# A four-layer graph network: ten of the sixteen diagonal blocks in the last layer, and one accumulator pool shared by the last two layers

## The chip, the cores and the metric

The kernel runs on one core of a Trainium2 chip. The metric is the device time of one execution in microseconds; the kernel before takes 1385.57 us (median of three runs, 1384.66 to 1387.64). A change of less than 0.2% (2.8 us) is about what these measurements cannot tell from none.

## The reference, cut to what matters

The input is x (4096 nodes, 64 features) and a symmetric, sparse adjacency matrix adj (4096 x 4096). Four layers follow one another, each of the form `x = layernorm(x + layer(x, adj))`: a polynomial in adj, an attention layer with two gated cells, a decay layer, and a hyperbolic layer. The change touches the last two.

```python
# layer 2 (decay): weight by the number of non-zeros that follow in the row
support = x @ weight
mask = (adj != 0)
rank = cumsum(mask, axis=1); deg = rank[:, -1:]; k = minimum(deg, 100)
pos = rank - (deg - k)
w = mask * where(pos > 0, 0.5 ** (k - pos), 0.0)
out = w @ support + bias

# layer 3 (hyperbolic)
log_ij = logmap(x[:, None, :], x[None, :, :])      # for every pair of nodes
agg = einsum('ij,ijc->ic', adj / deg, log_ij)
transformed = agg @ weight + bias
out = expmap(0, transformed)                        # needs the norm of each row of transformed
```

In the last layer a pair (i, j) needs one scalar factor f(i, j), which the kernel gets from a product of the two nodes' features by a square, three logarithms and exponentials and a few elementwise steps. The factor is symmetric, f(i, j) = f(j, i).

## The kernel before, in words

Nodes are cut into blocks of 128 (`P`) and groups of four blocks, 512 nodes (`GW`); there are 32 blocks and 8 groups. A shared scheduler places the instructions of each engine; `in_order` and `behind` pin the order of those that they name. Buffers come from pools. A pool in PSUM, the matrix engine's result memory, has a number of buffers for each tile name, and the framework adds the waits by which a buffer is not overwritten while it is read.

**The decay layer** (L1455 to L1549). A step counts, for 64 columns of the mask and 512 rows of each of four groups, how many non-zeros follow, and turns each count into a power of two. The loop at L1497 runs over 64 half-blocks `h`, and it is gone through twice (`turns_of`, four groups each), so there are 128 steps, or 64 pairs of an odd and an even step. One step does this:

- for `a` in 0, 1: two matmuls (`r` in 0, 1) of the constant `follow` with the mask write the two partition halves of the count tile `cnt[a]` (L1506); then `cnt[a]` is read out of PSUM into `wt[odd][a]`, by ACT (L1511) for `a == 0`, and for `a == 1` by ACT while there is work of the previous layer or turn to do beside it (`busy`), else by DVE (L1513);
- after these four matmuls come the gathers of earlier steps (L1514): at odd `h` the eight `gather_two` matmuls (L1466), at even `h` the eight `gather_lo` matmuls (L1478). They multiply the weights by the features into four accumulators `acc`.
- at even `h` one step of `seam` follows, a list of small steps of the neighbouring layers (products, transposes, layer norms).

PE runs its instructions in the order in which they stand: count pair `a = 0`, count pair `a = 1`, gathers, then the next step. The two count tiles are two separate tiles of the pool `ps_c2`, `cnt_ps0` and `cnt_ps1`, each 128 x 512 in fp32 with one buffer. After the last step the remaining gathers are run (L1547) and the accumulators are copied out (L1536).

**The last layer** (L1568 to the end). 36 tiles (i, j) of two groups each cover the upper triangle of the matrix of groups, the eight diagonal ones included. A tile is worked in two units `n` of two blocks by 512 columns (128 x 1024 values), so there are 72 units. The functions for a unit are `product` (L1613, PE into the PSUM tile `v_ps`, for even n from the pool `ps_v3`, for odd n from `ps_u3`), `square` (ACT, L1635), `less_one` (DVE, L1657), then in the loop Ln and Exp on ACT (L1866, L1867), `opposite` (PE, L1646), a step on DVE from `v_ps` (L1889), a third Exp and a second Ln on ACT (L1891, L1900), the factor f on DVE (L1876), and its product with the adjacency tile on DVE (L1879). `gather` (L1694, L1706) multiplies the weighted tile by the features. For a tile off the diagonal, `turn` transposes f on PE (L1678) and DVE multiplies the transposed blocks with the mirrored adjacency tile (L1680).

On a diagonal tile (i = j) `columns` makes the second unit half as wide: of the sixteen 128 x 128 blocks the first unit computes eight (two rows of four), the second the four at the lower right. The four at the lower left are transposes of four of the first unit, made by one `turn` (L1671, L1673) one unit later.

When a group's sums are complete, its end is added to `seam` by `finals` (L1770): small steps `first` to `fifth`, one each unit. `third` (L1804) takes the squared norms of the rows with four ACT squares of 64 columns that also sum (L1808). The last two groups' ends stand after the last unit.

Of the kernel before, what the change touches and what calls it, by code (L numbers as in the profile page):

```python
# [9 lines left out]
F32 = mybir.dt.float32  # L10
# [50 lines left out]
def gnn4_kernel(  # L61
# [153 lines left out]
    def in_order(ins):  # L215
        return tc.keep_in_program_order(ins)

    def cols(b):
        return slice(b * P, (b + 1) * P)
# [1171 lines left out]
    def behind(engine, ins):  # L1391

        if engine in begun:
            tc.add_manual_dep(
                ins.ins, begun[engine],
                mybir.DependencyInfo(mybir.DependencyClass.NoSync, mybir.DependencyReason.DATA),
                reason="behind",
            )
        begun[engine] = ins.ins.name
# [52 lines left out]
            lambda ps_p, g=g: turn_prepared(ps_p, g) for g in two  # L1452
        ]

    with tc.tile_pool(name="mask2", bufs=3) as mk_p, tc.tile_pool(name="wt2", bufs=3) as wt_p, tc.tile_pool(  # L1455
        name="ps_c2", bufs=1, space=PSUM
    ) as ps_c, tc.tile_pool(name="ps_p2", bufs=2, space=PSUM) as ps_p, ExitStack() as ps_a_open:

        def masks2():
            return [mk_p.tile([P, CB, GW], MASK, name=f"m{n}") for n in range(2 * QG)]  # L1460
# [24 lines left out]
        gathers = []  # L1485
        busy = True
        for turn, groups in enumerate(turns_of):
            cnt = [ps_c.tile([P, GW], F32, name=f"cnt_ps{a}") for a in range(2)]
            if turn:
                acc = [ps_a.tile([P, GW], F32, name=f"acc_ps{q}") for q in range(QG)]  # L1490
                to_right, to_other, spread, wh_x = constants3()
# [5 lines left out]
            for h in reversed(range(2 * NB)):  # L1497
# [29 lines left out]
                ]  # L1527
                lo = [lambda half=half, jb=jb, wt=wt, acc=acc: gather_lo(jb, half, wt, acc) for half in (1, 0)]

                gathers += lo + two if jb == 0 else two + lo  # L1530
                if jb == 0:
                    def copies(ps_p, acc=acc, groups=groups, turn=turn):
# [32 lines left out]

    with tc.tile_pool(name="ps_v3", bufs=1, space=PSUM) as ps_v, tc.tile_pool(  # L1568
        name="ps_p3", bufs=3, space=PSUM
    ) as ps_p, tc.tile_pool(name="ps_u3", bufs=1, space=PSUM) as ps_u, tc.tile_pool(name="o3", bufs=1) as op, tc.tile_pool(name="cols3", bufs=3) as cols_p, tc.tile_pool(  # L1570
        name="w3", bufs=4
    ) as wp3, tc.tile_pool(name="el3", bufs=3) as el, tc.tile_pool(name="f3", bufs=2) as fp, tc.tile_pool(
        name="r3", bufs=2
    ) as rp, tc.tile_pool(
        name="ps_a3", bufs=1, space=PSUM
    ) as ps_a:
        HB = CB // 2

        tb = op.tile([P, N], F32, name="tb")
        two_w = op.tile([P, 2 * F], F32, name="two_w")  # L1580
        spread_w = two_w[:, F : 2 * F]
        kappa = op.tile([P, 2, NB], F32, name="kappa")

        tiles = [(i, j) for n, i in enumerate(seq) for j in seq[n:]]
        NT = len(tiles)
        own, mirrored = {}, {}
        nc.gpsimd.memset(tb[F:P, gcols(seq[0])], 0.0)
        for g in seq[1:]:
# [11 lines left out]
                mirrored[t] = cols_p.tile([P, CB, GW], F32, name="at_m", tag="atm")  # L1600
                nc.sync.dma_start(mirrored[t], adj_t[j][:, i * CB : (i + 1) * CB, :])

        def columns(n):

            i, j = tiles[n // 2]
            return slice(2 * P if i == j and n % 2 else 0, GW)

        sums, fs = {}, {}
        ros.append(op.tile([P, GW], BF16, name="ro1"))
        vs, ws, rts = {}, {}, {}  # L1610
        NU = 2 * NT

        def product(n):  # L1613

            if n >= NU:
                return
            i, j = tiles[n // 2]
            vs[n] = (ps_u if n % 2 else ps_v).tile([P, HB, GW], F32, name="v_ps")
            cs = columns(n)
            for k in range(HB):  # L1620
                jb = j * CB + (n % 2) * HB + k
                half = slice(jb % 2 * F, jb % 2 * F + F)
                ins = nc.tensor.matmul(  # L1623
                    vs[n][:, k, cs], lhsT=tr_c[half, jb // 2, :], rhs=rights[i][0][half, cs], start=True, stop=True
                )
                in_order(ins)
                if n < 2:
                    behind("PE", ins)

        def square(n):  # L1630
            if n >= NU:
                return
            ws[n] = wp3.tile([P, HB, GW], F32, name="w3")
            cs = columns(n)
            ins = nc.scalar.activation(ws[n][:, :, cs], vs[n][:, :, cs], AF.Square)  # L1635
            behind("ACT", ins)

        def opposite(n):
            if n >= NU:
                return  # L1640
            i, j = tiles[n // 2]
            cs = columns(n)
            for k in range(HB):
                jb = j * CB + (n % 2) * HB + k
                half = slice(jb % 2 * F, jb % 2 * F + F)
                ins = nc.tensor.matmul(  # L1646
                    vs[n][:, k, cs], lhsT=tr_o[half, jb // 2, :], rhs=rights[i][1][half, cs],
                    start=False, stop=True, skip_group_check=True,
                )
                in_order(ins)  # L1650
                if n < 1:
                    behind("PE", ins)

        def less_one(n):
            if n < NU:
                w = ws[n][:, :, columns(n)]
                ins = nc.vector.tensor_scalar(  # L1657
                    w, w, -SCALE * SCALE, V_FLOOR * (V_FLOOR + 2.0) * SCALE**2, ALU.add, ALU.max
                )
                behind("DVE", ins)  # L1660

        def turn(n):

            t, h = n
            i, j = tiles[t]
            work = []
            if i == j:
                tp = ps_p.tile([P, GW], F32, name="post", tag="post")
                for k in range(HB):
                    for b in range(HB):  # L1670
                        nc.tensor.transpose(tp[:, cols(HB * k + b)], fs[t][:, b, cols(HB + k)], ident)  # L1671
                to = own[t][:, HB:CB, 0 : HB * P]
                work.append(lambda: nc.vector.tensor_tensor(to, tp.rearrange("p (k i) -> p k i", k=HB), to, ALU.mult))  # L1673
                return work
            for b in (HB * h, HB * h + 1):
                tp = ps_p.tile([P, GW], F32, name="post", tag="post")
                for k in range(CB):
                    nc.tensor.transpose(tp[:, cols(k)], fs[t][:, k, cols(b)], ident)  # L1678
                to = mirrored[t][:, b, :]
                work.append(lambda to=to, tp=tp: nc.vector.tensor_tensor(to, tp, to, ALU.mult))  # L1680
            return work
# [88 lines left out]
        def finals(g):  # L1770
# [33 lines left out]
            def third(ps_p):  # L1804

                sq = sm.tile([P, GB, F], F32, name="sqv", tag="t0")
                for b in range(GB):
                    nc.scalar.activation(sq[:, b, :], v[:, b, :], AF.Square, accum_out=n[:, b : b + 1])  # L1808
                nc.vector.tensor_scalar_max(n, n, MIN_NORM * MIN_NORM)
                nc.scalar.activation(n, n, AF.Ln)  # L1810
                nc.scalar.activation(vn[:, :, 0], n, AF.Exp, scale=0.5)
                nc.scalar.activation(vn[:, :, 1], n, AF.Exp, bias=ln_two, scale=-0.5)
# [32 lines left out]
        for t in range(3):  # L1845
            load_own(t)
            load_mirrored(t)
        product(0)
        square(0)
        product(1)  # L1850
        less_one(0)
# [2 lines left out]
        while n < NU + 2 or turns or gathers:  # L1854
# [5 lines left out]
            if n < NU:  # L1860
                if n % 2 == 0:
                    fs[n // 2] = fp.tile([P, CB, GW], F32, name="f3")
                w, cs = ws[n][:, :, columns(n)], columns(n)
                rts[n] = el.tile([P, HB, GW], F32, name="rt3")
                rt = rts[n][:, :, cs]
                behind("ACT", nc.scalar.activation(w, w, AF.Ln))  # L1866
                behind("ACT", nc.scalar.activation(rt, w, AF.Exp, scale=0.5))  # L1867
                square(n + 1)
                opposite(n + 1)
            if n >= 2 and n - 2 < NU:  # L1870
                m = n - 2
                t, h = divmod(m, 2)
                cm = columns(m)
                hs = slice(h * HB, (h + 1) * HB)
                f, at = fs[t][:, hs, cm], own[t][:, hs, cm]
                behind("DVE", nc.vector.scalar_tensor_tensor(  # L1876
                    f, rts.pop(m)[:, :, cm], T_MAX, ws.pop(m)[:, :, cm], ALU.min, ALU.mult
                ))
                behind("DVE", nc.vector.tensor_tensor(at, at, f, ALU.mult))  # L1879
                diagonal = tiles[t][0] == tiles[t][1]  # L1880
                before = t - 1 if t and tiles[t - 1][0] != tiles[t - 1][1] else None
                gathers[n + 1] = (t, h, before)
                if diagonal and h == 0:
                    late_turns[n + 1] = (t, 0)
                if not diagonal and h == 1:
                    turns.setdefault(n + 1, []).append((t, 0))
                    turns.setdefault(n + 2, []).append((t, 1))
            if n < NU:
                behind("DVE", nc.vector.scalar_tensor_tensor(rt, vs[n][:, :, cs], (1.0 + V_FLOOR) * SCALE, rt, ALU.max, ALU.add))  # L1889
                product(n + 2)  # L1890
                behind("ACT", nc.scalar.activation(w, w, AF.Exp, scale=-0.5))  # L1891
            late = turn(late_turns.pop(n)) if n in late_turns else []
# [3 lines left out]
            for work in turned + late:  # L1896
                behind("DVE", work())
            if 0 < n <= NU:
                rt = rts[n - 1][:, :, columns(n - 1)]
                behind("ACT", nc.scalar.activation(rt, rt, AF.Ln, scale=1.0 / SCALE))  # L1900
            if n == NU - 6:
                seam += [ahead_of_last(g) for g in seq[-2:]]
# [60 lines left out]
```

## Time and profile before

| | us |
|---|---|
| Median of three runs | 1385.57 (1384.66 to 1387.64) |
| The profiled execution, its own time | 1386.67 |
| Its span, first to last instruction | 1384.9 |
| Decay layer, first count to first product of the last layer | 751.7 to 955.6 |
| Last layer's loop | 955.6 to 1357.0 |
| End of the last two groups | 1357.0 to 1384.9 |
| Busy over the whole span: PE, DVE, ACT | 1299.2 (94%), 1043.6 (75%), 810.5 (59%) |

Times in the trace are microseconds from the start of the span. PE is the matrix engine's multiplication and PEld its loading of weights, DVE the vector engine, ACT the scalar engine, POOL the general one, and SP issues DMAs. A timeline row gives start, duration, engine, line, operation, what is written and what is read, a count, and in brackets how long the engine had been idle and what ended that. Ends of matmuls are modelled, and they overlap one another. The 1.8 us between the span and the time of the profiled execution are its start and end outside the trace.

### The profile page before, as it was taken

How to read it: one execution, taken by the hardware profiler on the slowest of the kernel's cores; microseconds unless marked ns; L12 is line 12 of the kernel's file. 1: busy time of each engine (PE TensorE's matmuls, PEld its weight loads, DVE VectorE, ACT ScalarE, POOL GpSimd, SP SyncE). 2: the span in 40 equal slices, each digit the busy share in tenths (PEclk: the TensorE clock that was granted, in tenths of full speed). 3: DMA queues.
4: the chain of work that ended last, by engine and by line, in shares of the span. 5: the costliest groups of instructions: out<-in, count | busy, mean ns of one | idle time of the engine just before them, and what ended most of it. 6: DMA issues, size and time to landing. Idle time of an engine off the chain costs nothing.

```text
span 1384.9 us, 19115 instructions
## 1 busy us (share of the span) xinstructions
PE 1299.2 (94%) x6812; PEld 613.3 (44%) x6812; DVE 1043.6 (75%) x1952; ACT 810.5 (59%) x1346; POOL 113.4 (8%) x200
## 2 busy tenths in 40 slices
PE   9999999999999999999999999998889898988984
PEld 6655656565544334444444323333334333433442
DVE  7789899899444257788885223335999999999997
ACT  5544444343000115654424775756989999999994
POOL 3111111101123000010111000001000000000000
PEclk9999999999999999999999999999999999999997
DMA  9999999999799999999985755443245453444430
GB/s 352 386 412 409 400 413 409 410 404 393 285 378 372 389 417 375 422 366 345 328 313 188 230 173 183 151 155 150 106 171 206 165 210 153 186 156 186 159 119 12
DMA packets 108191, 382.16 MB, mean 276 GB/s; under 512 B 20276, under 2 KB 20280, under 8 KB 76472
## 3 DMA queue, kind: packets, MB, share of 16 engines
q1 hardware_dynamic: 90472, 297.03, 57.8%
q0 software_dynamic: 12736, 76.29, 13.3%
q10 hardware_dynamic: 4880, 7.54, 1.4%
q8 instruction: 56, 0.92, 0.3%
q14 instruction: 47, 0.39, 0.1%
HBM read 294.05 MB, written 85.20 MB: 274 GB/s over the span
## 4 chain that ended last, share of the span: by engine, by line
PE 58%; ACT 17%; DVE 15%; DMA 6%; issue 3%; ACTq 0%; DVEq 0%; SPq 0%
PE pass L578 7%; PE tp L742 5%; PE w_ps L578 5%; DMA raw<-in_adj_dram 5%; PE cnt_ps L1506 4%; PE a_last L1215 4%; PE pass L571 4%; PE acc_ps L1466 4%; PE a_ps L1215 4%; ACT rt L1867 3%; ACT w L1866 3%; PE wide_last L1206 2%; DVE rt L1889 2%; ACT w L1635 2%; PE h_ps L571 2%
## 5 line engine op out<-in xcount | busy, mean ns | idle before, releaser
L749 ACT COPY at<-tp 128x512 f32<-128x512 f32 x248 | 127.9, 598 | 120.8 <-issue 91.2
L1511 ACT ACTIVATE wt<-cnt_ps 128x512 uint16<-128x512 f32 x212 | 117.4, 595 | 65.2 <-PE cnt_ps L1506 62.7
L777 DVE TENSOR_REDUCE dpart<-raw 128x4 f32<-128x2048 f32 x64 | 145.4, 2273 | 4.0 <-DMA raw<-in_adj_dram 3.8
L1694 PE MATMUL sums_ps<-at_d,some 128*64 128x512 f32 x288 | 143.8, 618 | 3.7 <-DVE at_d L1673 1.3
L779 DVE TENSOR_REDUCE lows<-raw 128x1 f32<-128x2048 f32 x64 | 145.4, 2272 | 0.0
L742 PE MATMUL tp<-ident,raw 128*128 128x128 f32 x1024 | 128.8, 279 | 9.1 <-DMA raw<-in_adj_dram 9.0
L742 PEld LDWEIGHTS tp<-ident,raw 128*128 128x128 f32 x1024 | 113.3, 142 | 45.0 <-issue 37.8
L1706 PE MATMUL sums_ps<-at_m,some 128*64 128x512 f32 x224 | 108.4, 605 | 0.2
L578 PE MATMUL pass<-at,cheb_n 128*128 128x512 f32 x224 | 97.5, 593 | 0.5 <-DVE cheb_n L811 0.5
L1623 PE MATMUL v_ps<-some,tr_a 64*128 64x512 f32 (+1 forms) x288 | 79.1, 626 | 17.9 <-DVE rt L1889 17.2
L578 PE MATMUL w_ps<-at,cheb_n 128*128 128x512 f32 x200 | 91.0, 598 | 0.0
L1889 DVE SCALAR_TENSOR_TENSOR rt<-v_ps,rt 128x1024 f32<-128x1024 f32 x72 | 83.4, 1158 | 6.7 <-ACT rt L1867 6.5
L1876 DVE SCALAR_TENSOR_TENSOR f<-rt,w 128x1024 f32<-128x1024 f32 x72 | 83.5, 1159 | 5.4 <-ACT rt L1900 5.2
L1506 PE MATMUL cnt_ps<-m,follow 128*64 128x512 fp8e4 x480 | 82.0, 391 | 4.7 <-ACT wt L1511 2.2
L1879 DVE TENSOR_TENSOR at_d<-at_d,f 128x1024 f32<-128x1024 f32 x72 | 83.7, 1163 | 1.2
L1866 ACT ACTIVATE w<-w 128x1024 f32<-128x1024 f32 x72 | 72.2, 1003 | 10.3 <-DVE w L1657 10.0
L1513 DVE TENSOR_SCALAR wt<-cnt_ps 128x512 uint16<-128x512 f32 x44 | 30.4, 692 | 61.8 <-PE cnt_ps L1506 61.8
L1867 ACT ACTIVATE rt<-w 128x1024 f32<-128x1024 f32 x72 | 72.8, 1010 | 2.0
L1680 DVE TENSOR_TENSOR at_m<-post,at_m 128x512 f32<-128x512 f32 x112 | 72.6, 684 | 0.1
L1900 ACT ACTIVATE rt<-rt 128x1024 f32<-128x1024 f32 x72 | 72.2, 1003 | 0.4
L1891 ACT ACTIVATE w<-w 128x1024 f32<-128x1024 f32 x72 | 72.1, 1002 | 0.0
L1678 PEld LDWEIGHTS post<-ident,f 128*128 128x128 f32 x448 | 47.6, 141 | 52.9 <-issue 34.6
(428 smaller groups left out, 2291.9 us busy)
## 6 DMA issues: line engine op xcount, KB each, us to landing
at<-adj_t SPq DMA_DIRECT2D x119, 1024.0 KB, 8.4
raw<-in_adj_dram SPq DMA_DIRECT2D x64, 1024.0 KB, 13.6
adj_t<-at POOLq DMA_DIRECT2D x62, 1024.0 KB, 8.1
at_d<-adj_t SPq DMA_DIRECT2D x36, 1024.0 KB, 4.6
at_m<-adj_t SPq DMA_DIRECT2D x28, 1024.0 KB, 6.7
m<-mask_t SPq DMA_DIRECT2D x120, 128.0 KB, 2.8
m<-mask_t SPq DMA_DIRECT2D x60, 256.0 KB, 3.5
mask_t<-mask ACTq DMA_DIRECT2D x28, 256.0 KB, 7.1
```

The source lines that it names most:

```text
L578: in_order(nc.tensor.matmul(ps, lhsT=cheb_n[:, jb, k : k + 2, :], rhs=rhs, start=first, stop=last))
L742: in_order(nc.tensor.transpose(tp[:, cols(b)], raw[:, b, cols(k)], ident))
L749: nc.scalar.copy(at[:, k, :], tp)
L777: in_order(nc.vector.tensor_reduce(dpart[:, g, c, :], raw, AX.X, ALU.add))
L779: in_order(nc.vector.tensor_reduce(lows[:, n : n + 1], raw.rearrange("p b j -> p (b j)"), AX.X, ALU.min))
L1215: in_order(nc.tensor.matmul(ps[q * F : (q + 1) * F, :], lhsT=nat_a[:, c * CB + k, 0:F], rhs=of[q if signed else 0][:, k, :], start=(c == 0 ...
L1506: in_order(nc.tensor.matmul(cnt[a][r * HP : (r + 1) * HP, :], lhsT=follow, rhs=chunks[c][odd][2 * a + r][:, k, :], start=(h == 2 * NB - 1) ...
L1511: in_order(nc.scalar.activation(wt[odd][a], cnt[a], AF.Relu, scale=-128.0))
L1694: in_order(nc.tensor.matmul(bank[0:F, :], lhsT=nat_c[:, j * CB + k, :], rhs=own[t][:, k, :], start=(i == j and k == 0), stop=(j == seq[-1] ...
L1866: behind("ACT", nc.scalar.activation(w, w, AF.Ln))
L1867: behind("ACT", nc.scalar.activation(rt, w, AF.Exp, scale=0.5))
L1889: behind("DVE", nc.vector.scalar_tensor_tensor(rt, vs[n][:, :, cs], (1.0 + V_FLOOR) * SCALE, rt, ALU.max, ALU.add))
```

## The change

Three things are changed.

1. The two count tiles of the decay layer become the two halves of one tile of 128 x 2 x 512, of the same shape and name as the last layer's `v_ps`, and of the same pool, `ps_v3`, which now opens ahead of the decay layer and has one buffer. The first `product` of the last layer is put ahead of the decay layer's last `gather_two` matmuls.
2. On the diagonal tiles ten blocks of 128 x 128 are computed instead of twelve: seven in the first unit (the rows of blocks 0 and 1, from the diagonal on) and three in the second. They stand packed, so that the elementwise steps take 896 and 384 columns in place of 1024 and 512. The product with the adjacency tile is made with one DVE instruction for each of the two rows of blocks. The six blocks below the diagonal are transposed in three lots (`mirror`) of one, four and one block, and each lot is multiplied by DVE; the first two are placed one unit earlier than the one lot before (`late_turns`).
3. In `third` the four squares with sums become one square of 256 columns on ACT, and a sum by DVE.

```diff
+    HB = CB // 2
+    tiles = [(i, j) for n, i in enumerate(seq) for j in seq[n:]]
...
+    def parts_of(n):
+        i, j = tiles[n // 2]
+        if i != j:
+            return [(k, slice(0, GW), k * GW) for k in range(HB)]
+        if n % 2:
+            return [(0, slice(2 * P, GW), 2 * P), (1, slice(3 * P, GW), GW)]
+        return [(0, slice(0, GW), 0), (1, slice(P, GW), GW)]
+
+    def flat(t, n):
+        parts = parts_of(n)
+        k, cs, to = parts[-1]
+        return t.rearrange("p k i -> p (k i)")[:, parts[0][2] : to + cs.stop - cs.start]
...
+    def product(n):
...
+        vs[n] = (ps_u if n % 2 else ps_v).tile([P, HB, GW], F32, name="v_ps")
+        for k, cs, _ in parts_of(n):
...
+    ps_v = ctx.enter_context(tc.tile_pool(name="ps_v3", bufs=1, space=PSUM))
...
-            cnt = [ps_c.tile([P, GW], F32, name=f"cnt_ps{a}") for a in range(2)]
+            counts = ps_v.tile([P, HB, GW], F32, name="v_ps")
+            cnt = [counts[:, a, :] for a in range(2)]
...
+                if turn and jb == 0:
+                    lo.append(lambda: product(0))
                 gathers += lo + two if jb == 0 else two + lo
...
             if i == j:
-                tp = ps_p.tile([P, GW], F32, name="post", tag="post")
...
+                def mirror(blocks, to):
+                    tp = ps_p.tile([P, GW], F32, name="post", tag="post")
+                    for m, (b, k) in enumerate(blocks):
+                        nc.tensor.transpose(tp[:, cols(m)], fs[t][:, b, cols(k - b % HB)], ident)
+                    tp = tp[:, 0 : len(blocks) * P]
+                    if len(blocks) > 1:
+                        tp = tp.rearrange("p (k i) -> p k i", k=HB)
+                    work.append(lambda: nc.vector.tensor_tensor(to, tp, to, ALU.mult))
+
+                if h:
+                    mirror([(2, 3)], own[t][:, 3, cols(2)])
+                    return work
+                mirror([(0, 1)], own[t][:, 1, cols(0)])
+                mirror([(0, 2), (1, 2), (0, 3), (1, 3)], own[t][:, HB:CB, 0 : HB * P])
                 return work
...
-                for b in range(GB):
-                    nc.scalar.activation(sq[:, b, :], v[:, b, :], AF.Square, accum_out=n[:, b : b + 1])
+                nc.scalar.activation(sq, v, AF.Square)
+                nc.vector.tensor_reduce(n, sq, AX.X, ALU.add)
...
-        product(0)
         square(0)
...
-                behind("DVE", nc.vector.tensor_tensor(at, at, f, ALU.mult))
+                if diagonal:
+                    for k, cs, to in parts_of(m):
+                        at = own[t][:, h * HB + k, cs]
+                        behind("DVE", nc.vector.tensor_tensor(
+                            at, at, f[:, k, to - k * GW : to - k * GW + cs.stop - cs.start], ALU.mult
+                        ))
+                else:
...
-                if diagonal and h == 0:
-                    late_turns[n + 1] = (t, 0)
+                if diagonal:
+                    late_turns[n] = (t, h)
```

## The prediction

> **What bounds the kernel now.** I read the busy times by stage first, for the three stretches that the change touches.
>
> ```profile
> core 0: us, PE busy (x) PEld busy (x) DVE busy (x) ACT busy (x) POOL busy (x), PEclk, DMA share, GB/s
> 751.70:955.60 203.90, 197.11 (x1640) 69.27 (x1638) 68.12 (x223) 127.79 (x242) 6.03 (x15) 0.99 0.51 158
> 955.60:1357.00 401.40, 357.99 (x1685) 155.21 (x1681) 385.26 (x614) 385.54 (x534) 13.49 (x22) 0.98 0.44 170
> 1357.00:1384.90 27.90, 8.47 (x48) 4.54 (x47) 19.24 (x80) 11.45 (x55) 0.00 (x0) 0.74 0.07 14
> ```
>
> In the decay layer (first row) PE is busy 97% and DVE and ACT have room. In the last layer (second row) DVE and ACT are busy 96% each. So the decay layer lives by PE never waiting, and the last layer by two engines at once.
>
> Next the timeline, for one pair of decay steps:
>
> ```profile
> 939.35 0.62 PE L1506 MATMUL cnt_ps<-m,follow 128*64 128x512 fp8e4 x4
> 939.86 0.60 ACT L1511 ACTIVATE wt<-cnt_ps 128x512 uint16<-128x512 f32 x1 [0.97 <-PE cnt_ps L1506]
> 939.90 0.40 PE L1478 MATMUL acc_ps<-wt,over_lo 64*64 64x512 bf16 x1
> 940.02 0.69 DVE L1513 TENSOR_SCALAR wt<-cnt_ps 128x512 uint16<-128x512 f32 x1 [0.84 <-PE cnt_ps L1506]
> 940.51 0.66 PE L1506 MATMUL cnt_ps<-m,follow 128*64 128x512 fp8e4 x4
> 941.01 0.60 ACT L1511 ACTIVATE wt<-cnt_ps 128x512 uint16<-128x512 f32 x1 [0.56 <-PE cnt_ps L1506]
> 941.10 0.39 PE L1466 MATMUL acc_ps<-wt,over_two 64*128 64x512 bf16 x1
> 941.21 0.69 DVE L1513 TENSOR_SCALAR wt<-cnt_ps 128x512 uint16<-128x512 f32 x1 [0.50 <-PE cnt_ps L1506]
> ```
>
> All four count matmuls go out in a row, both read-outs overlap, and PE is at the gathers (939.90, 941.10) while they run. The next pair of steps begins at 942.07, so a pair takes 2.72 us. Where ACT reads both halves, PE does wait, as the chain of waits shows:
>
> ```profile
> 776.82 0.35 PE cnt_ps L1506 x2
> 777.25 0.17 ACT wt L1511
> 777.75 0.60 ACT wt L1511
> 778.39 0.41 PE cnt_ps L1506 x2
> 778.79 0.97 PE acc_ps L1466 x8
> ```
>
> A count pair starts 0.04 us after the read-out of its tile ends (778.35 to 778.39). Such a pair of steps takes 2.95 us (776.75 to 779.70).
>
> **The shared count tile.** The program of the changed kernel, as built, has the same instructions in the decay layer but other waits. Step by step:
>
> ```
> before   PE cnt0 <- ACT read of cnt0, step before     PE cnt1 <- ACT/DVE read of cnt1, step before
> after    PE half 0 <- ACT/DVE read of half 1, step before
>          PE half 1 <- ACT read of half 0, THIS step (128 of 128)
>          DVE read of half 1 <- ACT read of half 0, this step
> ```
>
> The framework now treats both halves as one thing. PE, ACT, PE, ACT or DVE come strictly one after another, and the gathers stand behind the second count pair in PE's queue, so they can't fill the first gap. From the rows above: first pair to ACT's start 0.51; the read-out 0.60; 0.04 to 0.05 to the second pair; from there either the second read-out and back (DVE 0.42 + 0.69 + 0.05 = 1.16; ACT 0.50 + 0.60 + 0.05 = 1.15) or the gathers (they start 0.31 after the second pair; `gather_lo` takes 0.61, so 0.92; `gather_two` 0.97, so 1.28), whichever is longer.
>
> - Even step: 0.51 + 0.60 + 0.05 + 1.16 = 2.32. Odd step: 0.50 + 0.60 + 0.05 + 1.28 = 2.43. A pair: 4.75, whoever reads the second half.
> - Before: 44 of the second read-outs are on DVE, so 22 pairs at 2.72 and 42 at 2.95, together 183.7 us. The stage took 203.9, so 20.2 are seam steps on PE, two table loads on ACT and the start.
> - After: 64 x 4.75 = 304.0, and of the 20.2 what doesn't fit into PE's 0.25 us of slack behind `gather_lo`: 10 to 25 (more than before if ACT's small operations now delay read-outs that PE waits for); I take 17. Stage 321, **+117** (+94 if a pair takes 4.5 with the 10, +141 if 5.0 with the 25).
>
> What is queued behind the waiting count pair: the gathers, and the seam's matmuls. SP's mask loads come later with the loop; they took a share of 0.51 of the DMA engines, so they stay hidden.
>
> [...] The waits are in the program whether needed or not, so I go by the rows.
>
> **Ten blocks.** A diagonal tile loses 256 columns on five ACT steps. Rows for 1024 and 512 columns (1058 and 629 ns at L1867) give 0.84 ns a column: 5 x 256 x 0.84 = 1.07 us a tile, 8.6 for eight. DVE: `less_one` 0.53 ns a column (688, 418), -0.14; f and L1889 at 1.05 ns, -0.27 each; the product with adj goes from 1222 + 691 ns to four instructions of 1280 columns, by the same slope and its offset of 0.16 us each, +0.05; two more small `mirror` products at 0.28 (from 416 ns for 256 and 684 for 512 columns), +0.56. Net -0.07 a tile: nothing. PE gains two transposes (about 0.28 us each) and is not the bound. `third`: four squares took 1.06 us in a row (1360.70 to 1361.76); one of 256 columns takes about 0.36 (the 256-column copy at L1765 362 ns), and the sum adds 0.41 on DVE (L1789, 412 ns). Six of eight groups lie in the loop: ACT -4.2, DVE +2.5.
>
> So ACT loses 12.8 us of 401, DVE gains 2. DVE has only some 16 us of idle time, in short waits on ACT, so it becomes the bound. Ends: -12.8 if ACT alone sets the pace, +8 if DVE does (+2) and if the gather one unit earlier waits for a `mirror` product each time (8 x 0.7, one 512-column product). I take **-3**, nearest to DVE's row.
>
> **Seam and end.** `product(0)` starts before the eight last gathers (954.70 instead of 955.58), but in the built order the square no longer follows ACT's two accumulator copies, which now stand between Ln and Exp: of 0.88 us I take **-0.4** (-0.9 to +0.6). At the end the last two `third` each turn 1.06 us of ACT into 0.77 of ACT and DVE: **-0.6** (-1.5 to +0.5).
>
> **Sum.** 117 - 3 - 0.4 - 0.6 = +113. The profiled execution took 1386.67, so 1499.7; the median of the runs is 1.1 lower: **1498.6**.
>
> **Rivals.**
> - *The clock drops* (0.13). With PE stalled 0.9 us in each step, its granted clock may fall. For: in the last layer the clock went down where PE was busy 3.0 us of 5, against: not where it was 3.5.
>
> ```profile
> 990.00:995.00 5.00, 3.48 (x20) 1.79 (x20) 5.00 (x13) 4.50 (x7) 0.00 (x0) 1.00 0.58 210
> 1080.00:1085.00 5.00, 3.04 (x12) 1.04 (x12) 4.50 (x6) 5.00 (x10) 0.00 (x0) 0.88 0.59 213
> ```
>
>   The new pair keeps PE busy about 3.3 of 4.75 us (0.40 + 1.45 and 0.40 + 1.09), which is 3.5 of 5, like the first row. At half clock the gathers double, +1.6 a pair, and the count pairs add 0.4: half of the layer so makes 32 x 2.0 = 64, 1563. [...]
> - *Not slower: the waits cost nothing* (0.02). If the read-out of half 0 were done by the time PE reaches half 1, the decay layer would stay and the rest would give 1386.67 - 4.0 - 1.1 = 1381.6. It decides below 0.03 us a step (4.0 / 128). Against it: 0.51 + 0.60 us lie between the two pairs, and nothing else is in PE's queue there.
> - *The seam's work fills the gaps* (0.10). If all of the 20.2 and the small ACT operations vanish into the new idle time and a pair takes 4.5, the stage is 288, +84, and the time 1466.
> - *The last layer takes ACT's whole gain* (0.05): -12.8 in place of -3, 1489.
>
> **How the numbers follow.** The serial count chain at full clock has 0.70, with 1498.6 and its own range of 1482 to 1516 (a pair of 4.6 to 4.9, the remainder 10 to 25). For 8 in 10 I reach down to just below the filled gaps (1466) and up to a third of the layer at half clock (21 x 2.0 = 43, 1541): 1462 to 1545; more of the layer at that clock, and the second rival, are left out. Slower by over 0.2% (2.8 us, about what a measurement of this kernel can tell from no change) has all but the second rival: 0.97; faster 0.02, same 0.01.
>
> **What would show it.** In the profile after: in the decay layer count matmuls in twos, each second pair ended by ACT's read-out, a period of about 4.75 us a pair, the stage near 321 us; PE busy there near 70% with the clock near 1.00; ACT's diagonal groups at 896 and 384 columns and a last loop a few us shorter than 401 with DVE the busier engine. The prediction is wrong if both count pairs still go out in a row, if the stage's pairs differ from 4.75 by more than 0.3, or if the granted clock in it is under 0.95.

## The result, and the profile after

The changed kernel takes 1588.76 us (median of four runs, 1583.44 to 1599.65) against 1386.12 us for the kernel before: a ratio of 1.147, with a 95% interval of 1.145 to 1.150. The prediction was 1498.6 with a range of 1462 to 1545, so the sign was right and the size was 90 us short. The profiled execution has a span of 1581.7 us, 196.8 more than before.

The busy times by stage, in the three stretches in which the prediction showed them for the kernel before (decay layer, last layer's loop, end):

```profile
751.70:1147.90 396.20, 300.26 (x1635) 89.50 (x1631) 68.97 (x224) 137.99 (x242) 6.66 (x16) 0.68 0.26 81
1147.90:1550.00 402.10, 366.00 (x1702) 158.25 (x1698) 382.59 (x648) 374.40 (x499) 13.78 (x22) 0.97 0.44 169
1550.00:1581.70 31.70, 11.48 (x55) 5.98 (x55) 20.35 (x86) 9.79 (x35) 0.00 (x0) 0.71 0.06 13
```

The columns are the stretch, its length, then busy time and count for PE, PEld, DVE, ACT and POOL, the granted clock (its share of full speed), the DMA share and GB/s. The decay layer went from 204 to 396 us. Its column of the granted clock holds the surprise: 0.68, where the stage had 0.99 before. PE's busy time rose from 197 to 300 us for the same matmuls. The last layer, from which ACT was to lose 12.8 us, is no shorter.

Two groups of the changed kernel's page show the new chain of waits (count, busy time in us and mean of one in ns, then the idle time ahead of it and what ended it):

```profile
L1553 ACT ACTIVATE wt<-v_ps 128x512 uint16<-128x512 f32 x212 | 126.6, 597 | 247.8 <-PE v_ps L1548 247.4
L1548 PE MATMUL v_ps<-m,follow 128*64 128x512 fp8e4 x480 | 131.6, 534 | 85.3 <-ACT wt L1553 81.8
```

The count matmuls in the kernel before:

```profile
L1506 PE MATMUL cnt_ps<-m,follow 128*64 128x512 fp8e4 x480 | 82.0, 391 | 4.7 <-ACT wt L1511 2.2
```

They waited 4.7 us in all, 2.2 of them for the read-out, and took 391 ns each. Now they wait 81.8 us for it, and take 534 ns. The timeline of the changed kernel late in the layer, one pair of steps:

```profile
1130.92 0.64 PE L1548 MATMUL v_ps<-m,follow 128*64 128x512 fp8e4 x2
1131.60 0.60 ACT L1553 ACTIVATE wt<-v_ps 128x512 uint16<-128x512 f32 x1 [3.12 <-PE v_ps L1548]
1132.25 0.64 PE L1548 MATMUL v_ps<-m,follow 128*64 128x512 fp8e4 x2 [0.69 <-ACT wt L1553]
1132.82 0.63 PE L1519 MATMUL acc_ps<-wt,over_lo 64*64 64x512 bf16 x1
1133.00 0.69 DVE L1555 TENSOR_SCALAR wt<-v_ps 128x512 uint16<-128x512 f32 x1 [3.03 <-PE v_ps L1548]
1133.82 0.64 PE L1548 MATMUL v_ps<-m,follow 128*64 128x512 fp8e4 x2
...
1137.54 0.64 PE L1548 MATMUL v_ps<-m,follow 128*64 128x512 fp8e4 x2
```

The order is the predicted one: first half, ACT's read-out, second half, gathers, and then the next step. But the pair takes 6.62 us (1130.92 to 1137.54), not 4.75. A gather's matmul takes 0.63 us, which was 0.40. The clock in stretches of 10 us shows when this set in:

```profile
850.00:860.00 10.00, 6.95 (x56) 2.17 (x51) 0.00 (x0) 4.89 (x9) 1.31 (x3) 1.00 0.17 43
860.00:870.00 10.00, 6.79 (x38) 1.87 (x37) 0.00 (x0) 4.18 (x7) 0.00 (x0) 0.67 0.59 188
870.00:880.00 10.00, 7.81 (x36) 1.86 (x35) 0.00 (x0) 3.57 (x6) 0.00 (x0) 0.50 0.00 0
...
960.00:970.00 10.00, 8.57 (x38) 2.08 (x37) 5.18 (x20) 3.08 (x6) 1.21 (x3) 0.50 0.21 62
970.00:980.00 10.00, 9.15 (x67) 4.81 (x69) 3.73 (x20) 5.29 (x11) 0.62 (x2) 0.87 0.47 151
```

For the first 110 us of the layer the clock is mostly full (0.94 in the mean). Then it falls to 0.50 and stays there for 100 us, with PE busy 7.4 to 9.3 of 10 us. At the seam between the two turns, which has matmuls of its own, it comes back for 40 us, with short falls (0.83 to 1.00 in the stretches from 970 to 1010 us). From 1020 us to the layer's end it is 0.50 again, but for one of these stretches (0.67 from 1100 to 1110 us).

### The profile page after: what moved, and what is told of

Its sections match the earlier page's. It is cut to its first block, busy times and chain, and to the rows that moved or that the text cites. A ratio compares the mean times of both kernels' runs of the same rounds, so it can differ in the third digit from the quotient of the medians.

```text
span 1581.7 us, 19135 instructions
## 1 busy us (share of the span) xinstructions
PE 1412.5 (89%) x6828; PEld 636.7 (40%) x6828; DVE 1042.0 (66%) x1992; ACT 807.4 (51%) x1290; POOL 113.0 (7%) x200
## 3 DMA queue, kind: packets, MB, share of 16 engines
q0 software_dynamic: 12736, 76.29, 11.7%
## 5 line engine op out<-in xcount | busy, mean ns | idle before, releaser
L1553 ACT ACTIVATE wt<-v_ps 128x512 uint16<-128x512 f32 x212 | 126.6, 597 | 247.8 <-PE v_ps L1548 247.4
L1548 PE MATMUL v_ps<-m,follow 128*64 128x512 fp8e4 x480 | 131.6, 534 | 85.3 <-ACT wt L1553 81.8
L1507 PE MATMUL acc_ps<-wt,over_two 64*128 64x512 bf16 x256 | 100.9, 533 | 0.0
L1507 PE MATMUL acc_ps<-wt,sup_two 64*128 64x512 bf16 x256 | 100.6, 534 | 0.0
L1489 PE MATMUL v_ps<-some,tr_a 64*128 64x512 f32 (+3 forms) x288 | 80.0, 620 | 20.1 <-DVE rt L1917 17.2
L1896 DVE SCALAR_TENSOR_TENSOR f<-rt,w 128x1024 f32<-128x1024 f32 (+1 forms) x72 | 81.1, 1126 | 3.7 <-ACT rt L1928 3.6
L1917 DVE SCALAR_TENSOR_TENSOR rt<-v_ps,rt 128x1024 f32<-128x1024 f32 (+1 forms) x72 | 81.1, 1127 | 2.2 <-ACT rt L1888 2.2
L1887 ACT ACTIVATE w<-w 128x1024 f32<-128x1024 f32 (+1 forms) x72 | 70.5, 979 | 13.7 <-DVE w L1670 13.3
L1649 ACT ACTIVATE w<-v_ps 128x1024 f32<-128x1024 f32 (+1 forms) x72 | 67.8, 942 | 10.0 <-PE v_ps L1489 9.1
L1888 ACT ACTIVATE rt<-w 128x1024 f32<-128x1024 f32 (+1 forms) x72 | 71.0, 987 | 2.1
```

Of the source, the lines that this page charges most:

```text
L1507: in_order(nc.tensor.matmul(acc[2 * a + r], lhsT=(sup_two if r == half else over_two)[rows, jb, :], rhs=wt[half][a][rows, :].bitcast(BF16) ...
L1548: in_order(nc.tensor.matmul(cnt[a][r * HP : (r + 1) * HP, :], lhsT=follow, rhs=chunks[c][odd][2 * a + r][:, k, :], start=(h == 2 * NB - 1) ...
L1553: in_order(nc.scalar.activation(wt[odd][a], cnt[a], AF.Relu, scale=-128.0))
L1896: behind("DVE", nc.vector.scalar_tensor_tensor(flat(f, m), flat(rts.pop(m), m), T_MAX, flat(ws.pop(m), m), ALU.min, ALU.mult))
L1917: behind("DVE", nc.vector.scalar_tensor_tensor(rt, flat(vs[n], n), (1.0 + V_FLOOR) * SCALE, rt, ALU.max, ALU.add))
```

## The ledger

Counted from the first count to the first square (L1635 before, L1649 after: the first ACT row of the last layer), from there to the last square, and to the end:

| us, profiled executions | before | after | difference | predicted |
|---|---|---|---|---|
| up to the first count | 751.7 | 752.4 | +0.7 | |
| first count to first square | 205.0 | 397.6 | +192.6 | +117, and -0.4 for the seam |
| first to last square | 391.5 | 391.9 | +0.4 | -3 |
| last square to end | 36.6 | 39.8 | +3.1 | -0.6 |

## Experiments

**The changed kernel with two count tiles, and the kernel before with one.** My theory: everything that was lost lies in the waits between the halves and in the clock that falls with them.

```diff
 # e1_two_tiles, from the changed kernel (the pool ps_c2 and the place of ps_v3 are also as before)
-            counts = ps_v.tile([P, HB, GW], F32, name="v_ps")
-            cnt = [counts[:, a, :] for a in range(2)]
+            cnt = [ps_c.tile([P, GW], F32, name=f"cnt_ps{a}") for a in range(2)]
...
-                if turn and jb == 0:
-                    lo.append(lambda: product(0))
...
+        product(0)
         square(0)
 # e2_one_tile, from the kernel before
-            cnt = [ps_c.tile([P, GW], F32, name=f"cnt_ps{a}") for a in range(2)]
+            counts = ps_c.tile([P, 2, GW], F32, name="cnt_ps")
+            cnt = [counts[:, a, :] for a in range(2)]
```

> The changed kernel, but the two counts are two tiles again, in their own pool, and product(0) stands in its old place: the ten blocks, the fixed order and the reduce in the third step are left. Theory A (all of the loss comes from the waits between the halves of the one tile and from the clock that falls with them): the decay layer is back at 204 us (203.9 before, 396.2 after) with the clock at 0.99, and the whole is 1386 plus what the last layer itself changes; from the end of the accumulators to the end after took 430.7 us and before 429.3, so 1387. As predicted, with 12.8 us of ScalarE's work gone from the layer and all but 2 of the rest hidden: 1375. Rival (the layer was held back in the changed kernel only by the half clock at its start): also about 1375.

> [...] Last layer, pools' sharing and product(0) are as before. Theory A (the waits alone, and the clock they bring down): the decay layer takes about 396 us, mean clock about 0.68, counts in pairs with a ScalarE read between; the whole about 1386 + 192 = 1578. Rival (the half clock comes from the early product or the shared pool): the layer takes the predicted 321 us at a clock near 1.00; the whole about 1503. Rival (the waits cost little by themselves): under 1420.

e1_two_tiles: 1382.41 us, ratio 0.9967 (0.9952 to 0.9981). e2_one_tile: 1594.89 us, ratio 1.148 (1.144 to 1.152). The one tile alone, with nothing else of the change, makes all of the loss. Without it and the early product the rest of the change is a gain of 0.3%, and so e1_two_tiles is the fastest kernel of this study; its decay layer takes 202.9 us from the first count to the first square (205.0 before) at a clock of 1.00. Both expectations missed in size. The first lies between its two theories (taken up below). The second came out 17 us above 1578, which was reckoned from the profiled execution of the changed kernel, the fastest of its four: in the trace of e2_one_tile the clock is at 0.50 from 779 to 813 us, comes back, and is at 0.50 again from 854 us on, 10 us earlier than in the changed kernel. Its mean in the layer is 0.62, against 0.67. So the fall came at different times in these two kernels, and the times of the four runs of the changed kernel also go with the clock (spans of 1581.7 to 1597.9 at mean clocks of 0.905 to 0.887).

**Filling the gap.** This tells the chain of waits from the clock: the waits stay, and PE gets something to do in them.

The code is shortened: `live` holds the accumulators while they are open, and `fill` does nothing at other times.

```diff
+        zeros = const.tile([P, P], BF16, name="zeros")      # memset to 0
+        def fill():
+            for q in range(3):
+                rows = slice(q % 2 * HP, q % 2 * HP + HP)
+                in_order(nc.tensor.matmul(live["acc"][q], lhsT=zeros[rows, :],
+                    rhs=sup_two[rows, NB - GB : NB, :].rearrange("p b f -> p (b f)"),
+                    start=False, stop=False, skip_group_check=True))
...
                 for a in range(2):
                     for r in range(2): ...                   # the count pair
+                    if a == 0:
+                        fill()
```

> The changed kernel with three more matmuls of 512 columns in each step, between the pair of the first half and the pair of the second, where TensorE waits for ScalarE's read: their weights are zero, so they add zero to accumulators that are there anyway. The chain of waits is the same. Theory A (TensorE's idle time in the waits brings the clock down; the chain itself is 4.75 us per two steps): three matmuls of 0.21 us fit into the 0.7 us gap, the clock stays near 1.00, the decay layer takes 321 to 345 us, and the whole is 1513 to 1537. Rival (the clock falls for another reason, such as the work of the chip as a whole, or idle time that these three do not fill): the clock falls to 0.50 again, each of them takes 0.43 us, and the layer takes at least the 396 us of after; the whole 1589 or more.

1505.58 us (1502.04 to 1509.63), ratio 1.085 (1.081 to 1.088). Matmuls that add nothing but zero (369 in the trace) make the changed kernel 83 us faster. From the first count to the first square the layer takes 324.4 us (PE 286.8 busy, granted clock 0.98), as the theory had it; the whole came out 7 us under its 1513 to 1537, which were reckoned from the median of the changed kernel, while the 396 us of the layer were those of its fastest run. The timeline of e3_fill_between, one pair of steps:

```profile
1041.49 0.41 PE L1567 MATMUL v_ps<-m,follow 128*64 128x512 fp8e4 x2 [0.30 <-DVE wt L1576]
1041.83 0.60 PE L1512 MATMUL acc_ps<-sup_two,zeros 64*128 64x512 bf16 x3
1041.93 0.60 ACT L1574 ACTIVATE wt<-v_ps 128x512 uint16<-128x512 f32 x1 [1.76 <-PE v_ps L1567]
1042.58 0.41 PE L1567 MATMUL v_ps<-m,follow 128*64 128x512 fp8e4 x2 [0.15 <-ACT wt L1574]
...
1043.88 0.41 PE L1567 MATMUL v_ps<-m,follow 128*64 128x512 fp8e4 x2
...
1046.24 0.41 PE L1567 MATMUL v_ps<-m,follow 128*64 128x512 fp8e4 x2 [0.30 <-DVE wt L1576]
```

The pair takes 4.75 us (1041.49 to 1046.24), the predicted figure; most others take 4.74 to 4.85. So of the 192.6 us of the ledger, 119 are the chain of waits at a nearly full clock (324.4 less 205.0) and 73 are the clock.

**How much filling, and where.** Two theories of the clock are tried: that PE's busy share decides, and that the length of a single wait does. One kernel has one zero matmul in the gap. The other has all three, but behind the gathers, so that the gap itself stays empty.

```diff
 # e9_fill_one
-            for q in range(3):
+            for q in range(1):
 # e11_fill_behind
-                    if a == 0:
-                        fill()
...
                 for work in [gathers.pop(0) for _ in range(min(len(gathers), 4 if odd else 2))]:
                     work()
+                fill()
```

> e3_fill_between with one added zero matmul in each step in place of three. If TensorE's idle share decides on the clock, and any filling moves it: the clock falls for a part of the decay layer, which takes between 323 us (three, clock near 1.00 by the profile) and 396 us (none, 0.68). If the gap itself (0.7 us) matters and not its share: as none, the whole about 1589. If a single matmul is enough: as three, 1503 to 1508.

> e3_fill_between with the three zero matmuls of each step in another place: behind the step's gathers, so that the wait of the second count pair for ScalarE's read stays as long as in the changed kernel (0.78 us), while TensorE is about as busy as with one zero matmul in the gap (0.78 of the time). At full clock a step is 1.15 us to the second pair, then 0.31 to the gathers, 0.61 or 0.97 of gathers and 0.64 of zeros: 2.7 and 3.1, a pair 5.8, the decay layer 64 x 5.8 + 17 = 388 us, the whole about 1569. If TensorE's busy share decides on the clock: the clock stays near 1.00 but for short falls, and the layer takes 380 to 400 us. If waits of 0.78 us themselves bring it down: the clock falls to 0.50 for long stretches as in the changed kernel (0.67 mean), pairs take some 8 us there, and the layer takes over 450 us, the whole over 1630.

e9_fill_one: 1511.71 us (1506.95 to 1517.71), the layer 331.1 us at a clock of 0.95. e11_fill_behind: 1556.91 us (1555.12 to 1562.79), the layer 369 us at 0.98. The first lies between its theories, near that of the three. The second is under the 380 to 400 us expected: its pairs take 5.35 us (1040.20 to 1045.55) to 5.5, not the 5.8 that I worked out, because a step of gathers and zeros takes less than their sum. Sixty microseconds of the first turn in each: the changed kernel just before its clock falls for long, then e9_fill_one, e11_fill_behind and e3_fill_between.

```profile
800.00:860.00 60.00, 41.45 (x288) 13.53 (x285) 12.25 (x49) 30.87 (x55) 2.05 (x4) 0.94 0.30 96
```

```profile
860.00:920.00 60.00, 46.59 (x328) 17.35 (x326) 6.92 (x10) 23.88 (x40) 0.00 (x0) 1.00 0.37 115
```

```profile
860.00:920.00 60.00, 43.66 (x330) 13.64 (x330) 1.38 (x2) 24.99 (x42) 1.90 (x4) 1.00 0.30 90
```

```profile
860.00:920.00 60.00, 52.01 (x383) 17.71 (x375) 6.92 (x10) 24.22 (x41) 0.00 (x0) 1.00 0.36 115
```

PE is busy 69% in the first, and 3 us later its clock falls for 109 us; 78%, 73% and 87% in the others, and there it is full. The waits of e11_fill_behind for ACT's read-out are still there and as long as those ahead of the fall. A row of the changed kernel, 5 us before the fall, and one of e11_fill_behind:

```profile
858.25 0.41 PE L1548 MATMUL v_ps<-m,follow 128*64 128x512 fp8e4 x2 [0.69 <-ACT wt L1553]
```

```profile
1041.29 0.41 PE L1567 MATMUL v_ps<-m,follow 128*64 128x512 fp8e4 x2 [0.69 <-ACT wt L1572]
```

So a wait of this length did not bring the clock down for long by itself, and work in PE's idle time kept the clock up: 0.69 lost it after 111 us of the layer, 0.73 did not lose it for more than 3.5 us at a time between 770 and 1120 us. But PE's share alone does not order the kernels. e9_fill_one is the busier of the two, and has longer falls on both sides of the stretch shown, 10 us from 841 us and 14 us from 926 us:

```profile
840.00:850.00 10.00, 9.26 (x43) 2.54 (x39) 4.46 (x21) 4.05 (x9) 2.05 (x4) 0.53 0.47 147
930.00:940.00 10.00, 9.64 (x46) 3.45 (x45) 6.07 (x31) 3.43 (x8) 0.03 (x1) 0.52 0.00 0
```

Nor did a high share bring the clock back at once. In the changed kernel PE shows no gap from 948 to 958 us, and the clock stays at 0.50:

```profile
948.00:958.00 10.00, 10.00 (x44) 4.78 (x40) 3.45 (x8) 2.77 (x5) 0.00 (x0) 0.50 0.00 0
```

Which quantity decides, and where its line lies, is not shown by these runs.

**Product(0) back in its old place.** The last layer is no shorter in the changed kernel, while e1_two_tiles, which has the same layer, gains in it. The squares of the two run together from the sixth unit on, but the changed kernel is 6.1 us behind by then.

```diff
 # e6_fill_late_product, from e3_fill_between
-                if turn and jb == 0:
-                    lo.append(lambda: product(0))
...
+        product(0)
         square(0)
```

> e3_fill_between with one edit: product(0) is back in its old place, after the accumulators' last products and after the copies of them are issued. The one tile, the shared pool, the ten blocks and the reduce stay. Theory (the early product costs the seam: with it ScalarE and VectorE take the first unit's square, subtraction and logarithm ahead of the copies of the accumulators, and the next products and the end of the group wait for these copies; e3_fill_between needs 11.7 us from the first square to the third where e1_two_tiles needs 6.8, and stays 6 us behind from the fifth on): from the first square to the end 424 us as in e1_two_tiles, not 429.7; the whole 4 to 6 us under e3_fill_between, 1500 to 1502. Rival (the 6 us come from the shared pool or from where the banks lie): no change from 1505.6.

1502.96 us (1502.10 to 1505.94), ratio 1.085 (1.083 to 1.086). From the first square to the end it takes 423.9 us, as e1_two_tiles does (423.8), against 429.7 in e3_fill_between, and from the first count to the first square 324.5 against 324.4. So in the profiled executions the early product brings nothing ahead of the first square and costs 5.8 us behind it. The medians differ by 2.6 with ranges that overlap, and the ratios to the kernel before, run beside each, are the same (1.0845 and 1.0846), so the 4 to 6 us expected for the whole are not shown; the shift itself is in every profile. The third square comes 11.7 to 11.9 us after the first in three kernels with the early product (the changed one, e3, e9; in e11 9.9), and 6.8 in the five that have the same layer without it (e1, e4, e6, e7, e8). The rows of the changed kernel:

```profile
1150.97 0.63 DVE L1670 TENSOR_SCALAR w<-w 128x896 f32<-128x896 f32 x1 [4.05 <-ACT w L1649]
1151.51 1.28 DVE L1580 COPY sums<-acc_ps 128x512 f32<-128x512 f32 x2
1151.63 0.95 ACT L1887 ACTIVATE w<-w 128x896 f32<-128x896 f32 x1 [0.69 <-DVE w L1670]
1152.49 1.05 ACT L1580 COPY sums<-acc_ps 128x512 f32<-128x512 f32 x2
1153.60 1.22 PE L1489 MATMUL v_ps<-some,tr_a 64*128 64x256 f32 x4 [2.59 <-ACT sums L1580]
```

and of e6_fill_late_product:

```profile
1076.21 1.29 DVE L1599 COPY sums<-acc_ps 128x512 f32<-128x512 f32 x2 [1.24 <-PE acc_ps L1526]
1076.23 1.02 PE L1489 MATMUL v_ps<-some,tr_a 64*128 64x512 f32 x4
1076.43 1.07 ACT L1599 COPY sums<-acc_ps 128x512 f32<-128x512 f32 x2 [2.72 <-PE acc_ps L1526]
1077.65 0.67 PE L1489 MATMUL v_ps<-some,tr_a 64*128 64x256 f32 x4 [0.40 <-DVE sums L1599]
```

With the early product ACT and DVE take the first unit (1150.97, 1151.63) ahead of the copies. product(1) waits 2.59 us for these copies in place of 0.40, and the end of the group begins later too: its step L1424 on DVE starts 9.4 us after the first square, against 5.1. There is a second thing in these rows. After the longer wait the clock is down for 10 us. The 10.2 us that begin 3.6 us after the first square, in the changed kernel and then in e6_fill_late_product:

```profile
1153.60:1163.80 10.20, 10.20 (x40) 7.01 (x40) 4.97 (x22) 4.47 (x7) 1.85 (x5) 0.50 1.01 422
```

```profile
1080.90:1091.10 10.20, 6.80 (x32) 3.03 (x32) 9.74 (x32) 10.10 (x17) 0.12 (x1) 0.83 1.01 422
```

How much of the 5.8 us is the order of the queues and how much the slower PE, no run separates.

**The two edits of the last layer, one at a time.** e4_ten_blocks is e1_two_tiles with the old `third`; e5_third is the kernel before with the new one.

```diff
 # e4_ten_blocks, from e1_two_tiles (e5_third: the reverse, in the kernel before)
-                nc.scalar.activation(sq, v, AF.Square)
-                nc.vector.tensor_reduce(n, sq, AX.X, ALU.add)
+                for b in range(GB):
+                    nc.scalar.activation(sq[:, b, :], v[:, b, :], AF.Square, accum_out=n[:, b : b + 1])
```

> As e1_two_tiles, and the third step of the last layer's end again has its four ScalarE squares with a sum each in place of one square and a VectorE reduce: of the three changes only the ten blocks are left. If the reduce on VectorE is what takes the layer's gain away (in the changed kernel it stands behind the mirrored products, and the end took 31.7 us in place of 27.9), this is 3 to 5 us faster than e1_two_tiles; as predicted (the reduce saves some 0.6 us), it is within 1 us of it or slightly slower.

> The kernel before with one edit: the third step of the end of a group squares with one ScalarE instruction and sums with a VectorE reduce. As predicted for this edit (0.6 us less at the end; the steps inside the layer hidden): 1386. By the two runs that differ in it alone (1382.4 with ten blocks and the reduce, 1385.5 with ten blocks alone): 3 us less than before, 1383 to 1384. If the gain belongs to the two edits together, no change.

e4_ten_blocks: 1385.53 us, ratio 0.9990 (0.9974 to 1.0005), 3.1 us slower than e1_two_tiles, where the expectation had it at most slightly slower. e5_third: 1385.55 us, ratio 0.9988 (0.9975 to 1.0001): not the 1383 to 1384 reckoned from e4_ten_blocks, but no change, as for a gain of both edits together. Each alone can't be told from no change, and the two together gain 0.33%. Their sum, 0.22%, lies inside the interval of the pair (0.19% to 0.48%), so it stays open whether they help each other. In the profiles, one execution each, they add up: from the first to the last square the kernel before takes 391.5 us, e4_ten_blocks 388.0, e5_third 389.5 and e1_two_tiles 385.8, so 3.5 and 2.0 alone and 5.7 together. To the end e1_two_tiles gains 4.4 us on the kernel before (423.8 against 428.2 from the first square). That is a third of ScalarE's 12.8, and so its time lies between the two that its expectation gave.

**Which engine sets the pace of the last layer.** Work is added to one engine at a time, about as much as the ten blocks take from ACT.

```diff
 # e7_more_act, from e1_two_tiles; e8_more_dve in the same way, behind the operation that makes f
 # (the tile `again` is made beside the layer's other tiles)
+            if 0 < n <= NU and tiles[(n - 1) // 2][0] == tiles[(n - 1) // 2][1]:
+                behind("ACT", nc.scalar.activation(flat(again, n - 1), rt, AF.Ln, scale=1.0 / SCALE))
```

> e1_two_tiles with one more ScalarE logarithm of 896 or 384 columns for each half of a diagonal tile, into a tile that nobody reads: 8 x (0.94 + 0.52) = 11.7 us of ScalarE, about what the ten blocks take from it. If ScalarE sets the pace of the last layer (as the prediction had it: 12.8 us less on ScalarE give nearly as much), the whole grows by about 11 us, to 1393. If ScalarE has slack in these units and VectorE sets the pace (busy 374 of 386.1 us after the ten blocks, ScalarE 366.6): by 0 to 4 us, 1382 to 1386.

> e1_two_tiles with one more VectorE operation of 896 or 384 columns for each half of a diagonal tile, just behind the one that makes f, into a tile that nobody reads: 8 x (1.09 + 0.53) = 13.0 us of VectorE. If VectorE sets the pace of the last layer: the whole grows by about 12 us, to 1394. If ScalarE does: by 0 to 4 us, 1382 to 1386.

e7_more_act: 1387.76 us, 5.3 more than e1_two_tiles for 11.7 us on ACT. e8_more_dve: 1397.94 us, 15.5 more for 13.0 us on DVE. So DVE sets the pace for the most part, and ACT's work counts by less than half. The first lies between its two expectations. The second cost 2.5 us more than was added, and why was not looked into. The loop of e1_two_tiles, from the first product to 1340 us, fits that:

```profile
953.90:1340.00 386.10, 351.52 (x1659) 150.84 (x1657) 373.97 (x636) 366.58 (x484) 12.78 (x20) 0.99 0.47 176
```

DVE is busy 374.0 of 386.1 us. ACT lost 11.3 us against the kernel before (366.6, from 377.9 in the 392.7 us of that loop), DVE only 3.4.

**A try to go further.** If DVE's microseconds count by 1.2 and ACT's by 0.45, moving work from the one to the other should pay.

```diff
 # e10_relu, from e1_two_tiles; by_act: diagonal units of all groups but the first; edge holds the two biases
+                if by_act(n):
+                    behind("ACT", nc.scalar.activation(w, w, AF.Relu, bias=edge[:, 0:1]))
+                    return
...
-                behind("ACT", nc.scalar.activation(w, w, AF.Ln))
+                ln_bias = {"bias": edge[:, 1:2]} if by_act(n) else {}
+                behind("ACT", nc.scalar.activation(w, w, AF.Ln, **ln_bias))
```

> e1_two_tiles, and in the diagonal units of all groups but the first ScalarE does the subtraction and the floor: a Relu with a bias in place of VectorE's add and max, the floor added in the logarithm that follows. It computes the same. VectorE loses 7 x (0.63 + 0.35) = 6.9 us, ScalarE gets 7 x (0.92 + 0.49) = 9.9 us. By the two runs that added work to one engine each (13.0 us on VectorE cost 15.5, 11.7 us on ScalarE cost 5.3): 8.2 less and 4.5 more, so some 4 us under e1_two_tiles, 1378 to 1379. If the two engines take turns in setting the pace, or the Relu's place in ScalarE's queue delays the logarithm: no gain or a loss of up to 3 us, 1382 to 1386.

1393.32 us, ratio 1.0043 (1.0030 to 1.0056): 11 us slower than e1_two_tiles, a miss of both expectations. The group of f on DVE for the units off the diagonal, in e10_relu and then in e1_two_tiles:

```profile
L1906 DVE SCALAR_TENSOR_TENSOR f<-rt,w 128x1024 f32<-128x1024 f32 x56 | 68.2, 1218 | 13.3 <-ACT rt L1938 13.0
```

```profile
L1894 DVE SCALAR_TENSOR_TENSOR f<-rt,w 128x1024 f32<-128x1024 f32 x56 | 68.2, 1218 | 3.6 <-ACT rt L1926 3.4
```

The Relu of a diagonal unit stands in ACT's queue ahead of the logarithm that the f of the unit two before it needs, and DVE is idle 9.7 us more ahead of these f. A price taken from work added at the end of a queue's turn did not hold for work in the middle of it.

## Why the prediction was right and wrong

- **The waits, and the chain that they make: right.** Counts in twos, the second ended by ACT's read-out, and 4.75 us a pair at full clock (e3_fill_between: 4.75). The stage's predicted 321 us were the 324 of that kernel, seam and start included. All of the loss follows from the framework keeping the halves of one tile apart by waits (e2_one_tile): 119 us in the waits, 73 in the clock that fell with them.
- **"The serial count chain at full clock": the step that failed.** The sum took all 64 pairs at full clock. The mean clock in the layer was 0.67, and late in it a pair took 6.62 us. The rival that has the clock drop was named, but got 0.13 and half of a layer. Its price per pair was good (2.0 predicted; 6.62 less 4.75 is 1.87), its reach was not: 73 us of 1.87 each are 39 of 64 pairs. By the prediction's own bounds (the clock in the stage under 0.95, pairs more than 0.3 off 4.75) it is wrong.
- **How I came to doubt the drop.** I took one row of 5 us, PE busy 3.48 with the clock at 1.00, for a sign that this share holds the clock. One short stretch can't show that. In the changed kernel, too, shares of 0.65 to 0.77 went with a clock of 1.00 for 10 or 20 us at a time, and it fell in the end. The stall was misread as well: 0.9 us a step by the prediction, but 0.51 + 0.60 + 0.05 less the pair's 0.40 is 0.76, and the trace has 0.69 to 0.78. Once down, the clock stood at 0.50 for 109 us, and what makes it fall is not shown.
- **Whether the waits were needed** is not touched by any run. The framework's waits were there (81.8 us ahead of the count matmuls, ended by ACT's read-out), and a kernel of one tile without them was not tried.
- **Ten blocks and `third`, -3: right in kind.** DVE became the bound for the most part, as written, and ACT's 12.8 us mostly fell away. In e1_two_tiles the units gain 5.7 us, 4.4 to the end.
- **Seam, -0.4: wrong.** I saw that the square no longer follows ACT's copies, and counted only the 0.88 us by which it starts earlier. What was put behind it, the copies and with them product(1) and the end of the group, I did not follow; with the fall of the clock that came after it, it cost 6 us in the profile.
- **End, -0.6: wrong in sign, small.** 38.0 us in e1_two_tiles and 39.8 in the changed kernel against 36.6. The cause was not looked for.
- **The range** ended at a third of a layer at half clock. The rival at its own price came to 1563, so a range that took it in would have missed as well; with 39 pairs in place of 32, and the 6 us of the seam and the 3 of the end, it would have come near. All 64 pairs at its price (128 us, 1627) were the bound that the rows gave.

## What to carry to other kernels

Two halves of one tile were one tile to the framework here (e2_one_tile: 1594.89 us, ratio 1.148): before packing two results into one tile, look at who reads the first while the second is written. The new wait on the matrix engine had two prices, 119 us for the waits and 73 us for the clock that fell with them. Where a change leaves gaps in every step (here 0.7 us each, and a share of 0.69), price the whole stage at half clock as a case of its own (here the clock stood at 0.50 for 109 us from 863 us on). And when work is moved ahead in one queue, follow what it now stands in front of on the others (here 5.8 us).

## What was not expected of the hardware

- The clock fell for 109 us at 863 us although no wait of PE from 841 us on was longer than 0.8 us, with PE busy around 69%; that was 111 us after the start of the layer, and in e2_one_tile 102 us, after shorter falls.
- Once at 0.50, the longer matmuls (0.63 us in place of 0.40 for a gather's) made PE 74% to 93% busy, and the clock still stayed down, through 10 us without a gap in PE, until it came back at 973 us, in the seam. What brought it back is not shown.
- Idle work paid: a single 512-column matmul of zeros in each step was worth 77 us (1588.8 to 1511.7).
